# A hybrid block on one core: softplus of later groups summed by transfers, D h and the folding of partial sums left to transfers too, products back with tokens on partitions

## The chip, the cores and the metric

One core of one Trainium2 chip runs the whole program. The metric is the device time of one execution in microseconds, as the median of several runs. All data are fp32. The engines are PE (matrix products; PEld is its weight load), DVE (vector), ACT (scalar functions), POOL (here three kinds of work: a small power, and the issue of most DMAs), and SP (the other DMAs).

## The reference

The input x has 8 batches of 256 tokens with 128 features. Four blocks are added to it one after the other, each on a layer norm of x:

```python
x = x + _L0_attn_a_ref(_layernorm(x), ...)      # a selective-scan (Mamba-like) block
x = x + _L0_ffn_ref(_layernorm(x), ...)         # 8 experts, the best two of each token
x = x + _L0_attn_b_ref(_layernorm(x), ...)      # gated attention with squared relu
x = x + _L0_ffn_ref(_layernorm(x), ...)         # the same experts again
```

In the first block, 256 channels carry a state of 16 numbers each. After a projection, a convolution over 4 tokens and a SiLU that gives `h`, the recurrence is

```python
delta = jax.nn.softplus(ts @ dt_w + dt_b)
...
new = dA * state + d_t[:, :, None] * B_t[:, None, :] * h_t[:, :, None]
y = jnp.einsum('bin,bn->bi', new, C_t) + D * h_t
return (new, y * g_t)
...
return ssm @ out_w + out_b
```

The third block ends with `(u * attn_v) @ W_out + b_out`.

## The kernel before

The 8 batches are cut into four groups (0 to 3) of two batches, 512 tokens each. Most tiles have 128 features on partitions and a group's 512 tokens along the free dimension; x itself is held with tokens on partitions. A group passes through these steps, each a Python generator that yields one operation at a time:

- `prelude(g)` (named s): norm, transposes, projection `hid`, convolution, `h`, the projection `xpj` with B and C (which go through DRAM to be broadcast), and the softplus. That is built as relu(z) + ln(1 + e), e = exp(-|z|), with a correction of the rounding of 1 + e. In the tile `dl`, the relu (L569 on ACT; group 0 on DVE, L565) is joined by the correction (L587, L589) and the logarithm (L597), all on DVE; then `du` = dl * h (L598).
- `recurrence(g)` (m): 8 rounds q of 2 of the 16 state numbers, for each of two halves c of the channels. One such step is three DVE instructions over 128x1024: B du (L703), the scan (L708), times C (L712). ACT makes the decay exp(A delta) ahead (`feeder`, L658), which needs the exp table. From the second round on a step's result `st` is added to the first round's, `acc`, by a DMA that POOL issues (`adder`, L675). There are two `acc` and a ring of three `st`. Group 0's last two are left to PE instead. When all adds have landed, PE sums what is left in PSUM as `y` (L724 to L727): the skip D h by a diagonal matrix `skip_sb`, and each part by the identity; DVE multiplies with the gate into `du` (L730).
- `gating(g)` (g): the gate's projection and SiLU. `tail(g)` (t): `project_back` with `out_w`.
- `rest(g)` (r): experts (p), attention (a), experts again (r). An expert layer goes through 22 tiles of intermediate features: `gp` on PE, SiLU on ACT (`sg`), `up` on PE from x weighted by the token's share of the expert (`wb`), their product `it` on DVE (L925), and `dn` on PE (L931). The share of expert 0 is spread over the partitions by four products with the identity (L861); the others come as broadcast DMAs from DRAM (L894, POOL), followed by a multiplication on DVE (L902). Three `wb` buffers rotate.

`project_back` (and the end of an expert layer) makes features-on-partitions results of 512 columns, `pb`; `add_back` copies them to SBUF on ACT with the bias (`oT`, L451), turns them by four transposes on PE (`ot`, L458), and adds them to x on DVE (L461).

The order of the instructions on each engine is made by hand, before the program is built. Several such generators (lanes) are open at a time. `Board` keeps, in estimated microseconds, when each engine and each tile is free; `pick` takes the lane whose next operation can start first, and among lanes of the same engine that could start within PATIENCE of it the one with the lowest rank (`RANKS`; also estimates like `mm`, `act_us`, 0.2 for a transpose). A change of ACT's function table counts SWITCH more if the operation has been ready for less than LONG; with PATIENCE and LONG both 0 no wait is put up with to save a table load. When PE is expected to idle before a fresh accumulation, `do` writes filler products with the identity, one for each FILL = 0.23 us of the expected idle beyond 0.3 us (L307). Each engine executes its instructions strictly in that order, and waits on semaphores where an input isn't there. A DMA's wait is done by the queue that issues it (POOL or SP), and all that stands behind it on that queue waits too.

```python
for _ in range(int((idle - 0.3) / self.FILL)):
    op.fill()
```

Of the kernel before, what the change touches and what calls it, by code (L numbers as in the profile page):

```python
# [31 lines left out]
class Board:  # L32
# [3 lines left out]
    SWITCH = 1.3  # L36
    PATIENCE, LONG = 0, 0
    FILL = 0.23
# [56 lines left out]
def kernel(  # L95
# [27 lines left out]
    nc = tc.nc  # L123
# [25 lines left out]
    RANKS = {  # L149
        "s": [2, 4, 1.5, 2.5], "m": [3, 3.5, 3, 3.5],  # L150
        "g": [2, 2, 3.5, 2], "t": [1, 0, 3, 0],
        "r": [2.5, 1, 3.5, 1], "feeder": 5, "adder": 2.5,
    }
    SPLIT = ()
    ENDS = 2
# [37 lines left out]
    for name, src in (  # L193
        ("norm_scale", norm_scale.rearrange("(c p) -> c p", p=P)),
        ("in_b", in_b.rearrange("(c p) -> c p", p=P)),
        ("conv_w", conv_w.rearrange("k (c p) -> (k c) p", p=P)),
        ("conv_b", conv_b.rearrange("(c p) -> c p", p=P)),
        ("dt_b", dt_b.rearrange("(c p) -> c p", p=P)),
        ("D", D.rearrange("(c p) -> c p", p=P)),
        ("b_uv", b_uv.rearrange("(c p) -> c p", p=P)),  # L200
        ("gamma", gamma),
        ("beta", beta),
        ("out_b", out_b.rearrange("(c p) -> c p", p=P)),
        ("b_out", b_out.rearrange("(c p) -> c p", p=P)),
    ):
        n = src.shape[0]
        (nc.scalar if nrow % 2 else nc.gpsimd).dma_start(vecs[nrow : nrow + n, :], src)
        rows[name] = nrow
        nrow += n
# [32 lines left out]
    nc.sync.dma_start(b_v, b_uv[SE : 2 * SE].partition_broadcast(P))  # L242

    xs += [load_x(g) for g in range(1, NG)]

# [23 lines left out]
    one = const.tile([P, 1], FP, name="one")  # L269
    nc.vector.memset(one, 1.0)  # L270


# [25 lines left out]
    def shut(*held):  # L298
        for h in held:
            h.open = False  # L300

    def pe(us, out, ins, issue, fresh=True):
        def fill():
            ps = out[0].ap
            ps = ps if len(ps.shape) == 2 else ps.rearrange("p a b -> p (a b)")
            m, n = ps.shape[0], min(P, ps.shape[1])
            nc.tensor.matmul(ps[:, 0:n], lhsT=ident[:, 0:m], rhs=ident[:, 0:n], start=True, stop=True)  # L307

        return Op("PE", us, out, ins, issue, lag=0.25, fill=fill if fresh else None)
# [13 lines left out]
    def mm(n):  # L323
        return 0.06 + 0.00157 * n

# [101 lines left out]
    def transposed(xn, name, xT, scale=None):  # L427

        NT = xn.ap.shape[1]
        ps = bank([P, NT, P], f"tp_{name}")  # L430

        def turn():
            for t in range(NT):
                nc.tensor.transpose(ps.ap[:, t, :], xn.ap[:, t, :], ident)

        yield pe(0.2 * NT, [ps], [xn], turn)
        flat = ps.ap.rearrange("p t q -> p (t q)")
        yield act(act_us(NT * P), [xT], [ps], lambda: (
            nc.scalar.copy(xT.ap, flat) if scale is None else nc.scalar.mul(xT.ap, flat, scale)
        ))  # L440
        shut(ps)

    def add_back(x, psT, name, key, bias=None):
# [15 lines left out]

        yield pe(0.2 * NT, [ps], [oT], turn)  # L460
        yield dve(dve_us(NT * P), [x], [ps], lambda: nc.vector.tensor_add(x.ap, x.ap, ps.ap))  # L461
# [10 lines left out]

    def project_back(x, srcT, w_sb, bias, name, key):

        n = x.ap.shape[1] * P
        ps = bank([P, n], f"pb_{name}")
        yield pe(mm(n) * len(srcT), [ps], srcT, product(
            ps.ap, [(w_sb[:, c, :], s.ap) for c, s in enumerate(srcT)]
        ))
        yield from add_back(x, ps, name, key, bias)  # L480

# [3 lines left out]
    def prelude(g):  # L485

        GB = SIZES[g]
        G = GB * T
        xn = yield from layernorm(Held(xs[g]), f"m{g}", "m", rms=True, parts=xh[g])
        xT = ring(norm, [P, G], "xTm", f"xT_m{g}")  # L490
        yield from transposed(xn, f"m{g}", xT, scale=col("norm_scale"))


# [59 lines left out]

        dl = [ring(mam, [P, G], f"dl{c}", f"dl_{g}_{c}", bufs=2) for c in range(NI)]
        ex = ring(mam, [P, NI, G], "ex", f"ex_{g}")
        for c in range(NI):
# [11 lines left out]
            else:  # L568
                yield act(act_us(G), [dl[c]], [ps], lambda: nc.scalar.activation(  # L569
                    dl[c].ap, ps.ap, AF.Relu, bias=col("dt_b", c)  # L570
                ))
            shut(ps)

        parts = [(c, c + 1) for c in range(NI)] if g == 0 else [(0, NI)]
        exs = [Held(ex.ap[:, a:b, :], ex.ready) for a, b in parts]
# [26 lines left out]
        ww.used = max(w.used for w in wws)  # L602
        led_up[g] = bc, h, xT, dl, du

    def gating(g):
# [17 lines left out]
    fed = {}  # L623
    gone = {"du": 0, "scan": 0, "ct": 0, "sums": 0, "added": 0}
    sums = []

    def feeder():

        for g in range(NG):
# [6 lines left out]
            for q in range(N // NC):  # L636
# [12 lines left out]
                for c in range(NI):  # L649
# [16 lines left out]
                    das.append(da)  # L666

    def adder():

        while len(done & {f"m{g}" for g in range(NG)}) < NG:  # L670
            if not sums:
                yield None
                continue
            acc, st = sums.pop(0)
            yield load(6.3, [acc], [st], lambda: nc.gpsimd.dma_start(  # L675
                acc.ap, st.ap, accum_op=ALU.add
            ), "POOL", 0.9)
            st.used = acc.ready
            gone["added"] += 1

    def recurrence(g):
# [7 lines left out]

        acc, last = [], []  # L690
        for q in range(NQ):
            for c in range(NI):
                if q == 0:
                    st = ring(scan, [P, NC, G], f"acc{c}", f"acc_{g}_{c}")
                    acc.append(st)
                else:
                    while gone["added"] < gone["sums"] - 2:
                        yield None
                    st = ring(scan, [P, NC, G], "st", f"st_{g}_{q}_{c}", bufs=3)
                while len(fed.get((g, q), [[]])[-1]) <= c:  # L700
# [13 lines left out]
                if q == NQ - 1 and g == 0:  # L714
                    last.append(st)
                elif q > 0:
                    sums.append((acc[c], st))
                    gone["sums"] += 1
        while gone["added"] < gone["sums"] or g not in gates:
            yield None  # L720
        for c in range(NI):
            y = bank([P, G], f"y_{g}_{c}")
            parts = last[c : c + 1] + [acc[c]]

            yield pe(mm(G) * (NC * len(parts) + 1), [y], parts + [h[c]], product(
                y.ap, [(skip_sb[:, c, :], h[c].ap)]
                + [(ident, t.ap[:, n, :]) for t in parts for n in range(NC)]  # L727
            ))

            yield dve(dve_us(G), [du[c]], [gates[g][c], y], lambda: nc.vector.tensor_mul(  # L730
                du[c].ap, y.ap, gates[g][c].ap
            ))
            shut(y)

    def tail(g):
        gates.pop(g)
        bc, h, _, delta, du = led_up.pop(g)
        G = SIZES[g] * T
        yield from forked((RANKS["t"][g], g), [
            project_back(  # L740
                xh[g][p], of_part(g, p, du), out_w_sb, col("out_b"), f"m{g}{p}", f"y{p}"
            ) for p in range(len(PARTS[g]))
# [33 lines left out]
    def led_in(g, which, key, p, shared):  # L776
# [18 lines left out]

        yield pe(0.35 * NP, [lg], [xT], logits)

# [10 lines left out]
        if "we" not in shared:  # L808
# [8 lines left out]
            ]  # L817
            shared["wb"] = parted(g, ring(
                ffn, [P, NT * P], f"wb{key}", f"wb_{which}{g}_0", bufs=WB
            ))  # L820
        pair, we, wb = (shared[k][1][p] for k in ("pair", "we", "wb"))

# [32 lines left out]


        ps = bank([P, NP, P], f"we0_{nm}")

# [6 lines left out]

        yield pe(0.26 * NP, [ps], [we], spread)
        yield dve(dve_us(NP * P), [wb], [ps, xT], lambda: nc.vector.tensor_mul(
# [4 lines left out]
    def moe(g, which, key, shared, ends):  # L872
# [3 lines left out]
        G = NT * P  # L876
        xT, we, wb = (whole(*shared[k]) for k in ("xT", "we", "wb"))
        whole(*shared["pair"])
        sgs, wx, its = {}, {0: wb}, {}

# [23 lines left out]
        def up(i, cols_of, sg, wa, wn, it, width):  # L904
# [18 lines left out]

            yield pe(mm(width) + 0.3 * (cut < P), [ps], [wa] if cut >= P else [wa, wn], issue)
            yield dve(dve_us(width), [it], [ps, sg], lambda: nc.vector.tensor_mul(  # L925
# [10 lines left out]
        def tile_of(i):  # L936
# [3 lines left out]
        weT_ps = bank([E * NT, P], f"weT_ps_{nm}")  # L940
        yield pe(0.3, [weT_ps], [we], lambda: nc.tensor.transpose(
            weT_ps.ap, we.ap.rearrange("p e t -> p (e t)"), ident
# [11 lines left out]
        for i in range(LEAD):  # L954
            yield from gate(i)
        for e in range(1, WB):
            yield from fetched(e)
        yield from weighted(1)

# [47 lines left out]
    def attention(g, key, p, shared):  # L1007
# [20 lines left out]
        uT = [shared[f"uT{c}"][1][p] for c in range(NE)]  # L1028
        yield from transposed(xn, nm, xT)

        ps = bank([P, n], f"base_{nm}")
# [76 lines left out]
        for b in range(lo, hi):  # L1108
# [19 lines left out]
            shut(ps)  # L1128
        yield from project_back(xh[g][p], uT, wout_sb, col("b_out"), nm, f"{key}{p}")

# [28 lines left out]
    for g in range(NG):  # L1159
# [5 lines left out]
        waiting[-1].name = f"g{g}"  # L1165
        waiting.append(Lane((RANKS["t"][g], g), tail(g), [f"m{g}", f"g{g}"] + [f"t{g - 1}"] * (g > 0)))
        waiting[-1].name = f"t{g}"
# [59 lines left out]
```

## Time and profile before

| what | us |
|---|---|
| median of 3 runs (776.08 to 777.22) | 776.21 |
| the profiled execution | 775.3 |
| its span, first to last instruction | 773.5 |
| longest on the chain that ended last: `dn_r`, `gp_r`, `dn_p` on PE (10%, 9%, 8%); scan L708 on DVE (3%) | |
| DMA: 85.07 MB in all | |

In the lines below, a row of a group has: line, engine, operation, out<-in, shapes, count | busy us, mean ns of one | idle before it. A matrix product in fp32 leaves two PE records, which overlap their neighbours', so that the mean of one (about 600 ns for 512 columns) isn't its cost; the distance from one start to the next is. Some rows that the change touches:

```
L469 PE MATMUL y<-acc,ident 128*128 128x512 f32 x32 | 15.0, 592 | 0.0
L469 PE MATMUL y<-h,skip_sb 128*128 128x512 f32 x16 | 8.2, 593 | 0.0
L587 DVE SCALAR_TENSOR_TENSOR ex<-ww,ex 128x1024 f32<-128x1024 f32 x3 | 3.6, 1216 | 0.0
L589 DVE TENSOR_TENSOR dl<-dl,ex 128x512 f32<-128x512 f32 x8 | 5.3, 688 | 0.2
L597 DVE TENSOR_TENSOR dl<-dl,ww 128x512 f32<-128x512 f32 x8 | 5.4, 678 | 0.0
L57 ACT ACT_TABLE_LOAD x97 | 124.5, 1283 | 1.7
acc<-st POOLq DMA_DIRECT2D x54, 512.0 KB, 6.4
```

The last is of the table of DMA issues: 54 transfers of 512 KB, median 6.4 us from issue to landing.

### The profile page before, as it was taken

How to read it: one execution, taken by the hardware profiler on the slowest of the kernel's cores; microseconds unless marked ns; L12 is line 12 of the kernel's file. 1: busy time of each engine (PE TensorE's matmuls, PEld its weight loads, DVE VectorE, ACT ScalarE, POOL GpSimd, SP SyncE). 2: the span in 40 equal slices, each digit the busy share in tenths (PEclk: the TensorE clock that was granted, in tenths of full speed). 3: DMA queues.
4: the chain of work that ended last, by engine and by line, in shares of the span. 5: the costliest groups of instructions: out<-in, count | busy, mean ns of one | idle time of the engine just before them, and what ended most of it. 6: DMA issues, size and time to landing. Idle time of an engine off the chain costs nothing.

```text
span 773.5 us, 8167 instructions
## 1 busy us (share of the span) xinstructions
PE 745.8 (96%) x2967; PEld 393.5 (51%) x2967; DVE 565.1 (73%) x824; ACT 442.3 (57%) x580; POOL 108.6 (14%) x157
## 2 busy tenths in 40 slices
PE   4999999996999999999999999999999999999997
PEld 3877996652435754334554444344445434543443
DVE  2599998988997999899769898994642634263332
ACT  4688233797983896896956777742153232522221
POOL 2011110120210231211100222111010101010000
PEclk9999999998999999999999999999999999999999
DMA  8629792395863173847612748563010100011110
GB/s 257 195 71 224 179 227 94 86 212 127 215 157 95 54 175 104 191 121 164 161 30 70 176 122 211 146 146 69 2 41 14 41 29 27 14 29 40 28 42 14
DMA packets 33064, 85.07 MB, mean 110 GB/s; under 512 B 4132, under 2 KB 13952, under 8 KB 33024
## 3 DMA queue, kind: packets, MB, share of 16 engines
q0 software_dynamic: 12640, 43.13, 27.1%
q1 hardware_dynamic: 20336, 41.41, 16.4%
q8 instruction: 23, 0.38, 0.2%
q14 instruction: 17, 0.14, 0.1%
q10 hardware_dynamic: 48, 0.01, 0.0%
HBM read 54.79 MB, written 1.44 MB: 73 GB/s over the span
## 4 chain that ended last, share of the span: by engine, by line
PE 75%; DVE 16%; issue 3%; DMA 2%; ACT 2%; POOL 1%; DVEq 0%; POOLq 0%
PE dn_r L931 10%; PE gp_r L469 9%; PE dn_p L931 8%; PE gp_p L469 7%; PE y L307 7%; PE up_r L911 7%; PE up_p L911 6%; PE y L469 3%; DVE st L708 3%; PE up_r L918 3%; PE up_p L918 2%; DMA wb_p<-wrow_p 2%; DVE acc L708 2%; DVE st L703 2%; PE av_a L1116 1%
## 5 line engine op out<-in xcount | busy, mean ns | idle before, releaser
L708 DVE TENSOR_TENSOR_SCAN st<-decay,st 128x1024 f32<-128x1024 f32 x56 | 128.1, 2288 | 3.2 <-DVE st L703 0.5
L57 ACT ACT_TABLE_LOAD x97 | 124.5, 1283 | 1.7
L885 ACT ACTIVATE sg_r<-gp_r,zero 128x512 f32<-128x512 f32 x88 | 60.0, 685 | 112.0 <-PE gp_r L469 93.4
L658 ACT ACTIVATE decay<-dl,zero,a_sb 128x510 f32<-128x510 f32 x128 | 96.6, 805 | 38.1 <-DVE st L708 35.9
L925 DVE TENSOR_TENSOR it_r<-up_r,sg_r 128x512 f32<-128x512 f32 x88 | 60.1, 685 | 65.4 <-PE up_r L911 39.5
L885 ACT ACTIVATE sg_p<-gp_p,zero 128x512 f32<-128x512 f32 x88 | 59.5, 686 | 78.1 <-PE gp_p L469 49.9
L931 PE MATMUL dn_p<-it_p,wd_sb 128*128 128x512 f32 x176 | 92.2, 610 | 5.6 <-DVE it_p L925 5.6
L931 PE MATMUL dn_r<-it_r,wd_sb 128*128 128x512 f32 x176 | 90.2, 602 | 0.0
L469 PE MATMUL gp_p<-xT_p,wg_sb 128*128 128x512 f32 x176 | 89.9, 598 | 0.0
L469 PE MATMUL gp_r<-xT_r,wg_sb 128*128 128x512 f32 x176 | 89.6, 595 | 0.0
L925 DVE TENSOR_TENSOR it_p<-up_p,sg_p 128x512 f32<-128x512 f32 x88 | 59.8, 683 | 36.7 <-PE up_p L911 18.2
L675 POOL DMA_DIRECT2D acc<-st x54 | 47.3, 876 | 238.0 <-DVE st L712 213.1
L712 DVE TENSOR_TENSOR st<-st,ct 128x1024 f32<-128x1024 f32 x56 | 68.3, 1219 | 0.7
L703 DVE TENSOR_TENSOR st<-bt,du 128x1024 f32<-128x1024 f32 x56 | 68.1, 1216 | 0.0
L911 PE MATMUL up_p<-wb_p,wu_sb 128*128 128x512 f32 x128 | 65.5, 595 | 0.0
L911 PE MATMUL up_r<-wb_r,wu_sb 128*128 128x512 f32 x128 | 64.9, 594 | 0.0
L931 PEld LDWEIGHTS dn_p<-it_p,wd_sb 128*128 128x128 f32 x176 | 31.3, 191 | 49.8 <-issue 32.7
L469 PEld LDWEIGHTS gp_r<-xT_r,wg_sb 128*128 128x128 f32 x176 | 33.0, 190 | 43.3 <-issue 38.0
L469 PEld LDWEIGHTS gp_p<-xT_p,wg_sb 128*128 128x128 f32 x176 | 33.5, 192 | 42.0 <-issue 36.2
L307 PEld LDWEIGHTS y<-ident 128*128 128x128 f32 x468 | 52.7, 192 | 1.3 <-PE dt L469 0.8
L307 PE MATMUL y<-ident 128*128 128x128 f32 x468 | 53.0, 275 | 0.0
L931 PEld LDWEIGHTS dn_r<-it_r,wd_sb 128*128 128x128 f32 x176 | 31.5, 190 | 39.7 <-issue 36.1
(226 smaller groups left out, 904.2 us busy)
## 6 DMA issues: line engine op xcount, KB each, us to landing
acc<-st POOLq DMA_DIRECT2D x54, 512.0 KB, 6.4
bt<-bc SPq DMA_DIRECT2D x32, 512.0 KB, 5.9
ct<-bc SPq DMA_DIRECT2D x32, 512.0 KB, 4.6
wb_p<-wrow_p POOLq DMA_DIRECT2D x28, 256.0 KB, 4.0
wb_r<-wrow_r POOLq DMA_DIRECT2D x28, 256.0 KB, 3.6
wg_sb<-in_L_ffn_w_gate_dram SPq DMA_DIRECT2D x2, 704.0 KB
wu_sb<-in_L_ffn_w_up_dram SPq DMA_DIRECT2D x2, 704.0 KB, 5.9
wd_sb<-in_L_ffn_w_down_dram SPq DMA_DIRECT2D x2, 704.0 KB
```

Of the source, the lines that this page charges most:

```text
L57: self.load_tables(op.table)
L307: nc.tensor.matmul(ps[:, 0:n], lhsT=ident[:, 0:m], rhs=ident[:, 0:n], start=True, stop=True)
L469: nc.tensor.matmul(ps, lhsT=lhsT, rhs=rhs, start=(i == 0), stop=(i == len(terms) - 1))
L658: nc.scalar.activation(shaped[:, n, :, 1:], delta[c].ap.rearrange("p (b t) -> p b t", b=GB)[:, :, 1:], AF.Exp, bias=zero, scale=a_sb[:, c, ...
L675: yield load(6.3, [acc], [st], lambda: nc.gpsimd.dma_start(acc.ap, st.ap, accum_op=ALU.add), "POOL", 0.9)
L703: yield dve(1.22, [st], [bt, du[c]], lambda: nc.vector.tensor_mul(st.ap, bt.ap, du[c].ap.unsqueeze(1).to_broadcast([P, NC, G])))
L708: yield dve(2.29, [st], [das[c]], lambda: nc.vector.tensor_tensor_scan(flat, das[c].ap.rearrange("p n t -> p (n t)"), flat, 0.0, ALU.mult, ...
L712: yield dve(1.22, [st], [ct], lambda: nc.vector.tensor_mul(st.ap, st.ap, ct.ap))
L885: yield act(act_us(G), [sg], [gp], lambda: nc.scalar.activation(sg.ap, gp.ap, AF.Silu, bias=zero), SILU)
L911: nc.tensor.matmul(ps.ap, lhsT=wu_sb[:, i * P : (i + 1) * P], rhs=wa.ap[:, cols_of], start=True, stop=True,)
L925: yield dve(dve_us(width), [it], [ps, sg], lambda: nc.vector.tensor_mul(it.ap, ps.ap, sg.ap[:, cols_of]))
L931: yield pe(mm(dn.ap.shape[1]), [dn], [it], lambda: nc.tensor.matmul(dn.ap, lhsT=wd_sb[:, i, :], rhs=it.ap[:, cols_of], start=(i == 0), sto ...
```

## The change

1. In groups 1 to 3 the softplus is put together by two adding DMAs into one tile `both`: the correction `ex` and the logarithm `ww` are added to the relu by POOL's queue. ACT's identity now subtracts one and turns the sign, so that DVE makes the correction in one operation and the logarithm takes the scale -1.
2. In the same groups, ACT multiplies `h` by D in place after `du`, and a DMA of 256 KB adds it to the first state of `acc`. PE's skip product stays in group 0 alone.
3. In groups 2 and 3 (FOLD) a DMA adds the second half of each `acc` to the first, and DVE multiplies it with the gate from SBUF. Group 1 still sums its two halves on PE.
4. What stood at the end of `recurrence` becomes a lane of its own, `ending` (f), so that the next recurrence may begin before it. `acc` and `st` come from one pool of five states.
5. `project_back` makes its products with tokens on partitions: 8 products of 128 columns with the activations as weights, whose sum is added to x directly. `oT` and `ot` are gone there (not at the end of the expert layers). The biases are added to x early by POOL (`biased`), from two tiles that SP loads ahead of the x of groups 1 to 3.
6. The spread of expert 0's share by PE is kept only where SOON names the layer (p0, p1, r0, p3, r3); in p2, r1 and r2 it comes as a DMA like the others.
7. The planner: PATIENCE 0.21, LONG 3.0, new ranks, and new estimates for PE (`mm`, transposes 0.115 each, logits 0.205, spread 0.235, split `up` +0.14).

```diff
-    PATIENCE, LONG = 0, 0
+    PATIENCE, LONG = 0.21, 3.0
...
+        "s": [4, 1, 2.5, 2.5], "m": [1.5, 4, 3.5, 3.5],
+        "g": [4, 0, 3.5, 0], "t": [1, 3, 0, 0.5],
+        "r": [2.5, 1, 3.5, 3], "f": [1, 0, 0.5, 0], "feeder": 5, "adder": 0,
...
+    SOON = ("p0", "p1", "r0", "p3", "r3")
...
-        return 0.06 + 0.00157 * n
+        return 0.005 + 0.00167 * n
...
+    def biased(x, bias):
...
+        yield pool(1.2, [x], [], lambda: nc.gpsimd.tensor_tensor(
+            x.ap, x.ap, bias.unsqueeze(1).to_broadcast([P, NT, H]), ALU.add
...
+    def project_back(x, srcT, w_sb, name):
...
+            for t in range(NT):
+                for c, s in enumerate(srcT):
+                    nc.tensor.matmul(
+                        ps.ap[:, t, :], lhsT=s.ap[:, t * P : (t + 1) * P], rhs=w_sb[:, c, :],
+                        start=(c == 0), stop=(c == len(srcT) - 1),
+                    )
...
+        yield dve(dve_us(NT * P), [x], [ps], lambda: nc.vector.tensor_add(x.ap, x.ap, ps.ap))
...
+            yield act(act_us(NI * G), [ww], [ex], lambda: nc.scalar.activation(
+                ww.ap, ex.ap, AF.Identity, bias=minus_one, scale=-1.0
+            ))
+            yield dve(dve_us(NI * G), [ex], [ww], lambda: nc.vector.scalar_tensor_tensor(
+                ex.ap, ww.ap, 1.0, ex.ap, ALU.add, ALU.add
+            ))
+            sums.append((f"s{g}", 6.3, both, ex, both.ap, ex.ap))
+            yield act(act_us(NI * G), [ww], [], lambda: nc.scalar.activation(
+                ww.ap, ww.ap, AF.Ln, bias=zero, scale=-1.0
+            ), EXP)
+            sums.append((f"s{g}", 6.3, both, ww, both.ap, ww.ap))
+            while landed.get(f"s{g}", 0) < 2:
+                yield None
...
+                yield act(act_us(G), [h[c]], [], lambda: nc.scalar.mul(h[c].ap, h[c].ap, col("D", c)))
...
+                elif g > 0:
+
+                    sums.append((g, 4.5, acc[c], h[c], acc[c].ap[:, 0, :], h[c].ap))
...
+    FOLD = (2,3,)
+
+    def ending(g):
...
+        if g in FOLD:
+            for c in range(NI):
+                sums.append((g, 4.5, acc[c], acc[c], acc[c].ap[:, 0, :], acc[c].ap[:, 1, :]))
+                count += 1
+        while landed.get(g, 0) < count or g not in gates:
             yield None
         for c in range(NI):
+            if g in FOLD:
+                yield dve(dve_us(G), [du[c]], [gates[g][c], acc[c]], lambda: nc.vector.tensor_mul(
+                    du[c].ap, acc[c].ap[:, 0, :], gates[g][c].ap
+                ))
+                shut(acc[c])
+                continue
...
+            skip = [(skip_sb[:, c, :], h[c].ap)] if g == 0 else []
...
+        if not ahead:
+            yield from fetched(0)
```

## The prediction

> **What bounds the kernel now.** I read the page first. PE is busy 96% of the span, but line L307 is among its largest groups, and L307 is filler: products with the identity that the planner writes ahead of a PE operation it expects to wait (0.23 us of expected idle each). So I cut the span into five stages at landmarks of PE's timeline: the router weights of the first expert layer (p0) turned (151.8), p0's result turned back (239.9), the shares of p1 spread (271.2), group 3's product with `out_w` (540.6), the end. The first fence is the page, the second the table by stage (busy time and instruction count of each engine, granted clock, DMA share), the third the same for L307 alone.
>
> ```profile
> PE 745.8 (96%) x2967; PEld 393.5 (51%) x2967; DVE 565.1 (73%) x824; ACT 442.3 (57%) x580; POOL 108.6 (14%) x157
> ```
> ```profile
> 0.00:151.80 151.80, 139.40 (x953) 114.40 (x954) 122.32 (x152) 83.59 (x118) 19.77 (x40) 1.00 0.63 165
> 151.80:239.90 88.10, 78.90 (x246) 33.82 (x246) 78.68 (x75) 74.12 (x85) 15.78 (x21) 0.96 0.74 179
> 239.90:271.20 31.30, 30.25 (x159) 21.49 (x158) 27.98 (x66) 21.71 (x29) 6.34 (x4) 1.00 0.17 48
> 271.20:540.60 269.40, 268.68 (x871) 120.15 (x870) 237.25 (x316) 191.85 (x240) 48.06 (x64) 1.00 0.56 135
> 540.60:773.50 232.90, 228.60 (x748) 103.66 (x746) 98.87 (x218) 71.02 (x109) 18.60 (x29) 1.00 0.09 27
> ```
> ```profile
> 0.00:151.80 151.80, 96.99 (x831) 96.30 (x832) 1.00 0.63 165
> 151.80:239.90 88.10, 6.19 (x51) 6.09 (x52) 0.96 0.74 179
> 239.90:271.20 31.30, 8.22 (x68) 8.01 (x68) 1.00 0.17 48
> 271.20:540.60 269.40, 6.96 (x58) 6.95 (x58) 1.00 0.56 135
> 540.60:773.50 232.90, 1.32 (x8) 1.12 (x8) 1.00 0.09 27
> ```
>
> The reader is to see that until 271 PE waits for others (filler, and idle that shows at 151.8 to 239.9, where DVE and ACT are busiest), and that from 271 on PE is full of real work.
>
> PE executes its queue in order, filler included, so I count it. The timeline of PE gives the cadence: a product over 512 columns (two records) starts 0.86 us after the last, four transposes take 0.44, four 128-column products (eight records) 0.89, a filler 47.84/213 = 0.224.
>
> ```profile
> 441.87 0.60 PE L458 MATMUL ot_r<-ident,oT_r 128*128 128x128 f32 x4
> 442.31 1.02 PE L931 MATMUL dn_r<-it_r,wd_sb 128*128 128x512 f32 x2
> 443.17 1.02 PE L469 MATMUL gp_r<-xT_r,wg_sb 128*128 128x512 f32 x2
> 444.03 1.02 PE L911 MATMUL up_r<-wb_r,wu_sb 128*128 128x512 f32 x2
> ...
> 462.05 1.05 PE L861 MATMUL we_p<-ident,we_p 128*128 128x128 f32 x8
> 462.94 1.02 PE L911 MATMUL up_r<-wb_r,wu_sb 128*128 128x512 f32 x2
> ```
>
> At these cadences (256 columns 0.43, a split `up` 0.99) the program before holds 609.5 us of real PE work and 507 fillers, 112.9. The span of 773.5 leaves 51.1 in which PE does nothing: 19.1, 15.0, 2.5, 6.0 and 8.5 by stage. PE's share is therefore sharp; only the 51.1 must be guessed.
>
> **The change on PE.** The programs' order of instructions gives the counts. Sums of groups (`y`): 28 products of 512 columns become 14 (no D h in groups 1 to 3, no `y` in groups 2 and 3): -12.0. The transposes after `pb_m` and `pb_a` go, 32 at 0.11: -3.5. The products back become 64 of 128 columns (64 x 0.2225 = 14.2) for 16 of 512 (13.8): +0.5. Three of the eight spreads of the first share (L861) become transfers, 12 x 0.2225: -2.7. Real work 591.8, so -17.7. But the new planner writes 561 fillers, 54 more: 54 x 0.2225 = +12.0. They are executed whether or not the wait comes. Net -5.7. By stage, real + filler, before to after: 132.7 to 130.2; 73.1 to 69.6; 28.8 to 39.4; 263.4 to 264.2; 224.4 to 213.3.
>
> **The change elsewhere.** DVE loses, in each of groups 1 to 3, two subtractions and two additions of 512 columns (L589, L597: 688 and 678 ns), 2.7 us each; adds from PSUM after the products back replace those after the transposes, one for one. One such 2.7 us lies in stage 1 and one in stage 2, where DVE ends the waits; the third lies under PE. ACT loses 26 of 98 table loads at 1283 ns (33 us, from PATIENCE and LONG) and eight copies `oT` (687 ns), and gains six products h D (0.69, the row of the same shape). Ten of the loads and four decay instructions leave stage 2.
>
> Stage 2 is where this pays. The order before puts 14 recurrence steps there (1.22 + 2.29 + 1.22 = 4.73 us of DVE each), the new one 12: DVE 78.7 - 9.5 - 2.7 = 66.5, ACT 74.1 - 12.8 - 3.2 + 1.4 = 59.5, PE 69.6. The stage took 9.4 more than its busiest engine; 69.6 + 9.4 = 79.0. With the PE idle of 15.0 kept it is 84.6. I take 80, near the first, since every engine has slack then. What leaves is late next in stage 3: there the order shows 72 fillers for 34, ahead of `tp_a` and `we_p`, as I read it because the moved recurrence steps no longer cover p0's serial end and attention's start.
>
> Sum: stage 1 130.2 + 19.1 = 149.3; stage 2 80; stage 3 39.4 + 2.5 = 41.9; stage 4 264.2 + 6.0 = 270.2; stage 5 213.3 + 8.5 = 221.8. Together 763.2.
>
> **What before does not show.** (a) Eight adds of a bias on POOL, 128x512. From below the affine select of 128x128 on POOL, 285 ns, times 4 = 1.1 us; from above that plus the slowest row of POOL's tensor_tensor, 1727 ns (four elements, a power): 2.9. They wait for the last reader of x, and behind them stand adds and loads of the same queue. POOL is 14% busy; I take 0 for the end, at worst five of them (before 272) at 2.9 = 14.5. (b) Softplus: per group two adds of 512 KB to one tile. The second waits for the first to land (rows `acc<-st`: 4.5/6.4/9.8 us least, median, most), so POOL stands up to 9 us; behind it are queued the add of a recurrence state and, in stage 2, `wb_p` for expert 5. The order places the products du two to four steps later, and wb_p 5 is first read five rounds after its buffer comes free (5 x 80/22 = 18 us), so I take 0; at worst 9 each in stages 1 and 2, if DVE runs out of the five states. (c) D h by transfer is issued at a group's first step and hidden by the other seven. The folding add of groups 2 and 3 (256 KB; rows 3.3 to 9.2) comes after the last add and ahead of `du`; group 2's hides behind p1 and r0, group 3's tail is what the fillers of stage 5 (38 for 4) stand for. Counted. Removing everything could also pull stage 1 in by the slack of the recurrence's start (DVE waited 3.2 us for `y`), a gain of up to 3. (d) Traffic grows by 3 + 2.5 + 0.75 = 6.3 MB on 85.1.
>
> For all of these I add 1: 764.2. The profiled execution took 775.3 with a span of 773.5 (+1.8), and the median is 0.9 above it: **767**.
>
> [...] DVE's products with both operands in SBUF fill these stages (L703 and L712 1.22 us). [...]
>
> **The rivals.** *The relief goes further* (chance 0.18, 757): stage 2 comes down to 73 and attention starts before its fillers are through; 767 - 7 for the stage, - 3 for (c). For it: ACT loses 14.6 us there. Against: PE alone has 69.6.
>
> *The fillers do not replace idle, they are added to it, and the transfers are late* (0.14, 775): the 51.1 stays (span 767.8, so 770.5), plus one late wait of 4 to 5. For it: stage 5 was full of real work, and 38 fillers now stand in it. Then the change does little, 775 against 776.2.
>
> *Slower: POOL's queue stops the expert layers* (0.16, 782). The place is stage 2, later r0 and p1. Before, two late inputs there already cost PE this:
>
> ```profile
> 177.31 1.05 PE L918 MATMUL up_p<-wb_p,wu_sb 128*32 128x512 f32 x2 [3.37 <-DVE wb_p L902]
> ...
> 187.73 2.08 PE L931 MATMUL dn_p<-it_p,wd_sb 128*128 128x512 f32 x2 [3.92 <-DVE it_p L925]
> 189.60 1.91 PE L469 MATMUL gp_p<-xT_p,wg_sb 128*128 128x512 f32 x2
> 191.44 1.66 PE L918 MATMUL up_p<-wb_p,wu_sb 128*32 128x512 f32 x8
> ```
>
> After the second pause a product takes 1.87 (187.73 to 189.60) for 0.86, until 193.04, and the clock column falls to 0.96: 2.9 more. Together 3.4 + 3.9 + 2.9 = 10.2. The pair of softplus adds sits in the same queue as `wb_p` at the same place, with DMA already at 0.74. One more such burst brings 777, no change; the case decides from there, at one and a half it is 782, at two 787. Against: the landings of 8 to 9 us that caused it are already in the stage.
>
> **How the numbers follow.** Forecast 767 (0.52, 761 to 773). Within 0.2% of 776.2 (774.7 to 777.8) is about what a measurement of this kernel can't tell from no change. Faster: forecast 0.52 + relief 0.18 + 0.06 of the little case = 0.76; same 0.08; slower 0.16. The range 757 to 780 leaves out half of the relief case and most of the slow one, some 0.2, and reaches over the worst of (a) (767 + 13).
>
> **What would show it.** The span less real PE work and fillers stays near 50, with stage 2 at 77 to 85 us; the lines that follow L587 to L597 keep group 0's work and one operation for each later group; `y` keeps 14 products; table loads 72; no row in which ACT or DVE waits long for `dl`. Wrong would be: waits of `it` or `up` for `wb` beyond the 3.4 and 3.9 of before, DVE's first product of a step waiting for a landing, a POOL bias add over 3 us, or the clock column below 0.96 outside stage 2.

## The result and the profile after

The changed kernel takes 777.47 us (median of 12 runs, 772.93 to 779.3), the kernel before beside it 776.6 (775.1 to 777.37): ratio 1.0005, 95% interval 0.9986 to 1.0024. That is no change; 767 was forecast. The execution profiled after took 779.3 (span 777.3), the upper end of its runs, so its stages show some 2 us more than a median run would.

The first fence is the page's line of engines, the second the table by stage at the same landmarks as before (busy time and count of each engine, granted clock, DMA share), the third the fillers alone (now L326).

```profile
PE 744.7 (96%) x3087; PEld 404.9 (52%) x3087; DVE 567.4 (73%) x813; ACT 408.9 (53%) x552; POOL 136.0 (17%) x183
```
```profile
0.00:154.60 154.60, 138.47 (x940) 113.89 (x941) 122.08 (x148) 84.42 (x119) 27.34 (x46) 0.99 0.67 173
154.60:238.10 83.50, 75.73 (x232) 31.75 (x231) 69.00 (x67) 59.77 (x73) 15.85 (x21) 0.96 0.74 170
238.10:280.20 42.10, 41.79 (x261) 32.97 (x260) 38.83 (x80) 25.10 (x34) 13.49 (x9) 1.00 0.47 112
280.20:555.20 275.00, 270.97 (x892) 121.07 (x892) 242.38 (x310) 172.91 (x224) 57.91 (x75) 1.00 0.62 144
555.20:777.30 222.10, 217.76 (x771) 105.18 (x769) 95.14 (x210) 66.73 (x103) 21.40 (x32) 1.00 0.11 29
```
```profile
0.00:154.60 154.60, 94.68 (x810) 93.93 (x810) 0.99 0.67 173
154.60:238.10 83.50, 5.17 (x42) 5.19 (x43) 0.96 0.74 170
238.10:280.20 42.10, 16.98 (x144) 16.74 (x144) 1.00 0.47 112
280.20:555.20 275.00, 6.73 (x50) 6.52 (x50) 1.00 0.62 144
555.20:777.30 222.10, 9.64 (x76) 9.27 (x76) 1.00 0.11 29
```

The reader is to see that the work fell nearly as forecast (in stage 2 DVE from 78.7 to 69.0, with 66.5 forecast, ACT from 74.1 to 59.8, with 59.5 forecast), and that stage 2 still takes 83.5. Counted as in the prediction, real PE work is 591.7 us (forecast 591.8) and filler 124.5 (124.9). But the time in which PE does nothing grew from 51.1 to 61.1: by stage from 19.1, 15.0, 2.5, 6.0, 8.5 to 24.8, 14.0, 2.6, 10.8, 8.8. Stages 3 and 5 came out at 42.1 and 222.1 (forecast 41.9 and 221.8); stage 1 is 5.3 over the forecast, stage 2 3.5, stage 4 4.8.

This is one execution. Two runs below, x3 and f2, have the same instructions in the same order through stages 1 to 3; they took 154.4 and 155.2 in stage 1, 80.9 both in stage 2, 42.1 and 42.2 in stage 3. So the miss of stage 1 is firm, and that of stage 2 lies between 0.9 and 3.5.

What POOL's queue does in stage 1 is the next view, its timeline (start, time, what it waited for).

```profile
77.09 0.86 POOL L748 DMA_DIRECT2D dl<-ex  x1 [0.28 <-DVE ex L620]
86.47 0.86 POOL L748 DMA_DIRECT2D dl<-ww  x1 [8.52 <-ACT decay L729]
87.02 2.10 POOL L748 DMA_DIRECT2D st<-st  x2
96.71 0.87 POOL L748 DMA_DIRECT2D st<-st  x1 [7.59 <-DMA st<-st]
```

The second softplus transfer stands 8.5 us, until the first has landed (8.9 us from its issue), and the state adds leave behind it, two at once. (The releaser printed is ACT, whose `ww` was done at 78.0; the time is that of the landing. At 202.3 the same wait of 7.63 is printed as ended by DMA `dl<-ex`.) DVE, in order, then misses first `dl`, then a free state:

```profile
92.00 1.29 DVE L633 TENSOR_TENSOR du<-dl,h 128x512 f32<-128x512 f32 x2 [0.91 <-DMA dl<-ww]
96.20 1.23 DVE L776 TENSOR_TENSOR st<-bt,du 128x1024 f32<-128x1024 f32 x1 [2.90 <-DMA st<-st]
```

PE, which sums group 0's states at the end of this stretch, waits 4.3 us for one of them, and its products are slow behind that (5.34 us for eight records, 3.70 in x1 below; granted clock 0.86 from 120 to 132):

```profile
120.30 5.34 PE L488 MATMUL y<-st,ident 128*128 128x512 f32 x8 [4.25 <-DVE st L785]
```

The same stand is there at 193.8 (7.6 us) and 323.9 (7.6). In stage 2 PE's long pause is one of 5.7 us (3.4 and 3.9 in the kernel before), and slow products follow it (a product over 512 columns each 1.87 to 1.6, for 0.86):

```profile
179.88 1.93 PE L1025 MATMUL up_p<-wb_p,wu_sb 128*32 128x512 f32 x8 [5.71 <-DVE it_p L1032]
181.75 2.08 PE L1038 MATMUL dn_p<-it_p,wd_sb 128*128 128x512 f32 x2
183.62 1.75 PE L488 MATMUL gp_p<-xT_p,wg_sb 128*128 128x512 f32 x2
```

This pause ends at 179.9, ahead of the stand at 193.8, which so has no part in it; in x3 and f2 it is 4.3 and 4.0.

And a bias add on POOL stretches what DVE does beside it: the scan of 2.29 us takes 3.18.

```profile
46.66 1.65 POOL L495 TENSOR_TENSOR x<-x,b_first 128x512 f32<-128x512 f32 x1 [3.40 <-ACT xn_m L438]
```
```profile
47.27 3.18 DVE L781 TENSOR_TENSOR_SCAN st<-decay,st 128x1024 f32<-128x1024 f32 x1
```

The end of the scan less 2.29 is 48.16; POOL's add ends at 48.31. As an estimate from these two rows, the scan did next to nothing until the add was through. Six DVE instructions are stretched so, by some 6.5 us in all; in each, the end less the usual length falls 0.13 to 0.25 us ahead of the add's end.

### The profile page after: what moved, and what is told of

Same layout as the page of the kernel before. It is cut to its first block, busy times and chain, and to the rows that moved or that the text cites. A ratio compares the mean times of both kernels' runs of the same rounds, so it can differ in the third digit from the quotient of the medians.

```text
span 777.3 us, 8439 instructions
## 1 busy us (share of the span) xinstructions
PE 744.7 (96%) x3087; PEld 404.9 (52%) x3087; DVE 567.4 (73%) x813; ACT 408.9 (53%) x552; POOL 136.0 (17%) x183
## 3 DMA queue, kind: packets, MB, share of 16 engines
q0 software_dynamic: 15152, 49.69, 31.8%
## 4 chain that ended last, share of the span: by engine, by line
PE 56%; DVE 14%; DMA 13%; issue 5%; POOL 1%; ACT 1%; POOLq 0%; DVEq 0%
PE dn_r L1038 8%; PE gp_r L488 8%; PE dn_p L1038 7%; PE up_r L1018 6%; PE gp_p L488 5%; DMA wb_p<-wrow_p 5%; PE up_p L1018 5%; DVE st L781 3%; PE up_r L1025 3%; DVE st L776 2%; PE up_p L1025 2%; DVE st L785 2%; DMA st<-st 2%; DMA dl<-ex 2%; DMA wb_r<-wrow_r 2%
## 5 line engine op out<-in xcount | busy, mean ns | idle before, releaser
L781 DVE TENSOR_TENSOR_SCAN st<-decay,st 128x1024 f32<-128x1024 f32 x64 | 147.9, 2311 | 3.2
L748 POOL DMA_DIRECT2D st<-st x58 | 52.1, 920 | 229.0 <-DVE st L785 201.2
L776 DVE TENSOR_TENSOR st<-bt,du 128x1024 f32<-128x1024 f32 x64 | 77.9, 1218 | 2.9 <-DMA st<-st 2.9
L785 DVE TENSOR_TENSOR st<-st,ct 128x1024 f32<-128x1024 f32 x64 | 79.0, 1234 | 1.0
L326 PEld LDWEIGHTS y<-ident 128*128 128x128 f32 x414 | 46.6, 192 | 1.3 <-PE dt L488 0.8
L326 PE MATMUL y<-ident 128*128 128x128 f32 x414 | 46.8, 275 | 0.0
```

The costliest lines, as they stand in the source:

```text
L748: yield load(us, [acc], [st], lambda: nc.gpsimd.dma_start(into, of, accum_op=ALU.add), "POOL", 0.9)
L776: yield dve(1.22, [st], [bt, du[c]], lambda: nc.vector.tensor_mul(st.ap, bt.ap, du[c].ap.unsqueeze(1).to_broadcast([P, NC, G])))
L781: yield dve(2.29, [st], [das[c]], lambda: nc.vector.tensor_tensor_scan(flat, das[c].ap.rearrange("p n t -> p (n t)"), flat, 0.0, ALU.mult, ...
L785: yield dve(1.22, [st], [ct], lambda: nc.vector.tensor_mul(st.ap, st.ap, ct.ap))
```

## Theories

T: POOL's queue, standing 8 us for the second softplus transfer, makes states, `wb` and `du` late. R1: the bias adds cost, by DVE. R2: the 54 new fillers are pure cost. All experiments change the kernel after and keep the order of all other instructions, unless it is said. The stages are lengths in us of the profiled execution, at the same landmarks; the time is a median; the ratio is to the kernel before. Each stage length is of one execution: by the 83.5, 80.9 and 80.9 above, a difference of under 3 us in stage 2 shows little by itself, and the 12 runs of the kernel after spread over 6.4 us.

| run | stages 1, 2, 3, 4, 5 | time | ratio (95%) |
|---|---|---|---|
| after | 154.6, 83.5, 42.1, 275.0, 222.1 | 777.47 | 1.0005 (0.9986–1.0024) |
| x1 no softplus transfers | 149.7, 78.8, 42.2, 279.3, 222.1 | 773.67 | 0.9961 (0.9948–0.9974) |
| x2 no biases | 151.6, 79.7, 41.9, 274.5, 222.1 | 771.84 | 0.9950 (0.9938–0.9961) |
| x3 no late fillers | 154.4, 80.9, 42.1, 274.9, 226.3 | 780.78 | 1.0055 (1.0043–1.0068) |
| x4 all three | 149.0, 76.2, 41.8, 277.2, 226.4 | 773.80 | 0.9972 (0.9962–0.9982) |
| e1 no transfers, no biases | 148.7, 78.9, 41.8, 277.8, 222.2 | 770.66 | 0.9925 (0.9914–0.9937) |
| f1 one transfer | 153.9, 79.7, 42.1, 275.7, 222.2 | 775.39 | 0.9983 (0.9975–0.9992) |
| f2 all spreads on PE | 155.2, 80.9, 42.2, 278.7, 222.6 | 781.02 | 1.0052 (1.0035–1.0069) |
| f3 f1, biases on PE | 154.9, 78.6, 44.3, 279.8, 222.2 | 780.20 | 1.0047 (1.0033–1.0060) |
| f4 f3, all spreads | 154.1, 78.9, 44.3, 280.8, 222.6 | 784.12 | 1.0103 (1.0088–1.0117) |
| h1 softplus on DVE | 151.7, 80.0, 42.2, 279.5, 222.1 | 777.39 | 1.0019 (1.0009–1.0029) |
| h2 h1, biases on DVE | 158.3, 78.1, 44.1, 278.6, 222.5 | 783.58 | 1.0095 (1.0081–1.0109) |
| h3 h1, biases by transfer | 150.4, 79.7, 43.4, 274.7, 222.1 | 771.47 | 0.9935 (0.9921–0.9949) |
| h4 h2, 14 fillers | 157.4, 81.3, 43.9, 278.5, 222.5 | 785.14 | 1.0113 (1.0099–1.0127) |
| e2 biases by transfer | 152.1, 79.9, 42.0, 274.8, 222.1 | 773.24 | 0.9964 (0.9953–0.9975) |
| e3 h3, 14 fillers | 150.6, 82.5, 41.8, 276.6, 222.1 | 774.77 | 0.9971 (0.9960–0.9982) |
| e4 h3, `wb` first | 150.3, 80.0, 41.9, 273.7, 222.1 | 769.34 | 0.9908 (0.9896–0.9920) |

## Leaving the suspects out

x1, the softplus transfers:

```diff
-            yield load(us, [acc], [st], lambda: nc.gpsimd.dma_start(
+            yield load(us, [acc], [st], lambda: str(g).startswith("s") or nc.gpsimd.dma_start(
```

> The changed kernel without the six accumulating transfers of the softplus (dl <- ex, dl <- ww of groups 1 to 3 are not issued, so the two terms of softplus that they carry are left out); the order of all other instructions stays. Theory T (POOL's queue stands some 8 us three times while the second add waits for the first to land, and what is queued behind it, state adds and wb, comes late): the idle time of PE falls from 61.1 us to 50 to 54, stage 1 from 154.6 to 149 to 151, stage 4 from 275.0 to 270 to 272, DVE's waits of wb_p for a landing from 23.9 us to under 12; time 767 to 771. Rival R1 (the bias adds on POOL stretch DVE's instructions): less than 2 us gained, 775 to 778. Rival R2 (the late fillers are pure cost): no gain either, 775 to 778.

Stages 1 and 2 gained 4.9 and 4.7, to 149.7 and 78.8, beside forecasts of 149.3 and 80. T holds in stage 1: DVE waits neither for `dl` nor for a state any more, and of PE's wait 0.2 is left:

```profile
116.09 3.70 PE L488 MATMUL y<-st,ident 128*128 128x512 f32 x8 [0.24 <-DVE st L785]
```

In stage 2 the gain is 2.1 beside the 80.9 of the other executions, which is within their scatter. DVE's waits for `wb_p` came down from 23.9 to 14.1, not to under 12; in x3 and f2 they are 20.4 and 14.9 with the transfers kept. The time, 773.67, lies between T's range and that of the rivals, for stage 4 lost 4.3, which no theory expected. In its PE timeline the pause before the first `up_r` of group 1's second expert layer is 3.6 us (1.4 in the kernel after), and slow products follow it (1.86 and 1.71 from one start to the next, for 0.86):

```profile
428.43 2.07 PE L1018 MATMUL up_r<-wb_r,wu_sb 128*128 128x512 f32 x2 [3.64 <-DVE wb_r L1009]
430.29 1.91 PE L488 MATMUL gp_r<-xT_r,wg_sb 128*128 128x512 f32 x2
```

x2, the biases:

```diff
-        yield pool(1.2, [x], [], lambda: nc.gpsimd.tensor_tensor(
-            x.ap, x.ap, bias.unsqueeze(1).to_broadcast([P, NT, H]), ALU.add
-        ))
+        yield pool(1.2, [x], [], lambda: None)
```

> The changed kernel without the eight bias adds on POOL (both biases left out); the order of all other instructions stays. R1 (the bias adds stretch DVE's scans and products by some 6.5 us in all, and hold POOL's queue): 4 to 6 us gained, 771 to 773, with no scan above 2.4 us where a bias add ran. T: 0 to 2 us gained, 775 to 777, since stages 1 and 4 keep POOL's waits for dl <- ex. R2: nothing, 777.

5.6 us gained, at the upper end of R1's range; the scan at 45.6 takes 2.29 again. Stage 1 gives 3.0. Stage 2 gives 3.8, though no bias add lies in it: its pause is 3.0 instead of 5.7, but 2.6 of the 3.8 are what the same instructions differ by between executions.

x3, the late fillers (`fill` returns after its 498th call):

> The changed kernel with the 63 fillers after the start of the second attention layer not issued (498 of 561 stay); the order of all other instructions stays. R2 (these fillers are added to the idle time instead of standing in for it): 63 x 0.2245 = 14 us less, 762 to 765. T (most of them stand where PE would wait anyway): 2 to 6 us gained, 771 to 775, with PE's idle time after 238 us grown by 8 to 12 us. Were the clock to fall for want of them, slower than 778 with a granted clock below 0.99 after 280 us. R1: as T.

R2 is refuted for the late fillers: 3.3 us slower, the expectation's third case. (The 38 that are new in stage 3 were not left out.) Stage 4, with 25 fillers less, is unchanged; stage 5, with 38 less, is 4.2 longer. The windows of PE from 552 to 592, of this kernel and of the kernel after, show why (the last but two is the granted clock):

```profile
552.00:592.00 40.00, 33.47 (x122) 20.65 (x121) 19.26 (x62) 14.76 (x24) 6.59 (x8) 0.83 0.06 18
```
```profile
552.00:592.00 40.00, 39.89 (x207) 27.75 (x206) 21.76 (x68) 15.14 (x24) 6.60 (x8) 1.00 0.07 21
```

Without the fillers PE pauses 3.3 us at 554.7, and then runs at about half its pace until 571.9 (`base_a` to `v_a` 1.87 us for 0.97). The 38 fillers stand in for idle time, and with them the clock here is 1.00 for 0.83.

x4, the three edits together, and e1, the first two with all fillers kept:

> The changed kernel without the six transfers of the softplus, the eight bias adds and the 63 late fillers together (softplus terms and biases left out). If the costs are separate, the gains of the three runs before add up: by T 7 + 1 + 4, so 763 to 767; if all three theories hold in full, 8 + 5 + 14, 750. If a fourth cause is the larger one, less than 5 us is gained, 772 or more.

> The changed kernel without the softplus transfers and without the bias adds, all fillers kept (softplus terms and biases left out); the order of all else stays. If the transfers of the softplus and the bias adds are the whole of what the prediction missed, the stages come to its numbers: stages 1 to 3 at 149 + 76 + 42, stage 4 at 270 to 276, stage 5 at 222, so a span of 759 to 765 and a time of 761 to 767. If something else stops PE too (the late wb_r before the second expert layer of group 1, 3.8 us in the run without the transfers), stage 4 stays at 277 to 280 and the time at 766 to 770.

x4 fell outside both sums and into the last case (773.8): it also loses in stage 5, as x3 (226.4 and 226.3 for 222.1; mean clock of the execution 0.986 and 0.981 for 0.992). e1 says more: 770.66, its span 769.4 for the 764.2 worked out. Its stages 1, 2, 3 and 5 are below the forecast ones or within 0.4 of them (148.7, 78.9, 41.8, 222.2 beside 149.3, 80, 41.9, 221.8); the rest is stage 4, 277.8 for 270.2. So the two left-out things make up the miss in stages 1 to 3, nearly all of it in stage 1, and a third thing is in stage 4.

## Putting the work elsewhere

f1, one transfer in place of two:

```diff
+                if str(g).startswith("s") and landed.get(g, 0) == 0:
+                    held[g] = of
+                    return
+                if g in held:
+                    nc.vector.tensor_add(of, of, held.pop(g))
+                nc.gpsimd.dma_start(into, of, accum_op=ALU.add)
```

> The changed kernel with one transfer per group for the softplus: DVE adds the logarithm to the other term in SBUF (1.4 us for 1024 columns, three times), and the sum goes to dl by a single accumulating transfer, issued where the second stood; all other instructions keep their order. Theory T (the cost is POOL standing some 8 us for the landing of the first add): no DMA issue on POOL waits for dl <- ex any more; stages 1 and 2 together fall from 238.1 us to 229 to 232, as without the transfers (228.5) plus at most the two DVE adds; time 771 to 775, stage 4 between 271 and 280 by whether wb_r comes late there. Rival (it is the traffic of the softplus transfers or their place, not the wait): stages 1 and 2 stay above 235 and the time at 775 to 779.

2.1 us less. Stages 1 and 2 sum to 233.6, between T's 229 to 232 and the rival's 235. Stage 1 falls only to 153.9: POOL waits 9.6 us for DVE's sum instead, two state adds are still issued together behind it, and DVE waits 2.3 for a state. Half of the softplus traffic is gone and most of stage 1's loss is still there, which speaks for the stand and against the traffic.

h1, no transfer, both adds on DVE:

```diff
...
+                else:
+                    nc.vector.tensor_add(of, of, held.pop(g))
+                    nc.vector.tensor_add(into, into, of)
```

> The changed kernel with the softplus of groups 1 to 3 put together on DVE at the place of the second transfer (two adds of 1024 columns, 2 x 1.2 us in each of three groups) and no transfer for it; all other instructions keep their order. Theory T (POOL's queue and the late landings, not the work that DVE was relieved of, cost the time): DVE waits neither for dl nor for a state at 92 to 96 us; stage 1 at 151 to 153, as without the transfers (149.7) plus the adds, stage 2 at 79 to 81, time 771 to 775. Rival (the relief of DVE was worth what the change wanted, and the adds now cost the scan 2.4 us in each of stages 1 and 2 and more behind them): 776 to 779.

Stages 1 and 2 fall to 151.7 and 80.0, within T's ranges, though DVE has the work back. The time does not fall (777.39), as the rival said, but not for its reason: stage 4 is 4.5 longer, with a pause of 3.7 before the same `up_r`. In x1, x4, e1, h1, h2 and h4 that pause is 3.4 to 3.8; in after, x2, x3, f1, f3, h3, e2 and e3 1.0 to 1.5. POOL's timeline, here of x1, tells them apart:

```profile
419.21 0.88 POOL L748 DMA_DIRECT2D st<-st  x1 [5.96 <-DVE it_r L1032]
419.75 2.00 POOL L1001 DMA_DIRECT2D wb_r<-wrow_r  x3
```

Three `wb_r` loads stand behind a state add. In the long cases the add is released with DVE's next `it_r` (after 6.0 us), in the short ones with the state's own product (5.1). `wb_r` leaves 0.9 us later, beside SP's 512 KB load `bt`, and lands 2 us later. Why the release moves is not settled.

f2 returns the three spreads of first shares to PE (`SOON` names all eight layers; replanned):

> The changed kernel with the first shares of all eight expert layers spread by PE again (the three that the change gave to transfers are taken back: 12 products of 128 columns, 2.7 us of PE); written by the same planner, so the order after 390 us differs a little. Theory W (the three transfers make PE wait 1.5 us and more for the first up of the second expert layer of group 1 and the first of group 2, rows at 434.2 and 468.5): the two waits go, 3 us against 2.7, and the time stays within 775.5 to 778.5. Rival (PE has no slack there, the waits are only moved): 779 to 781.

The waits at 434 and 468 go, but another of 2.0, with 1.9 lost in slow products behind it, ends at 476.2; 781.02, as the rival had it. In f4, with f3's edits, that wait is 2.1, at full pace behind it:

> One transfer for the softplus, three first biases by PE, and all eight first shares spread by PE. T and W: the sum of the three, 766 to 771, so faster than both kernels; with the waits in stage 4 near 433 and 467 us gone and PE's idle time at 48 to 52 us. Rival: as the third kernel of this set or 1 to 3 us slower, since the spreads cost PE 2.7 us in its full stretch.

784.12. The expectation failed with f3, whose bias goes through PE:

```diff
+                if bias is not None:
+                    nc.tensor.matmul(
+                        ps.ap[:, t, :], lhsT=ones_row, rhs=bias[0:1, :], start=True, stop=False
+                    )
...
```

> As the kernel with one transfer, and the first bias of groups 0, 1 and 2 is added by PE in front of the product back (12 products of 1 row by 128 columns, 12 x 0.11 = 1.3 us) instead of by POOL; all other instructions keep their order. If the POOL adds in stage 1 cost what leaving all eight out gained there (3.0 of 154.6 us), it is 2 to 4 us faster than the kernel with one transfer: 767 to 772. Rival (the gain of leaving the biases out came from the five other adds or from chance in where PE pauses): within 1.5 us of the kernel with one transfer.

```profile
256.33 0.48 PE L507 MATMUL pb_m<-b_first,ones_row 1*128 1x128 f32 x2
256.75 0.71 PE L511 MATMUL pb_m<-out_w_sb,du 128*128 128x128 f32 x4
```

A one-row product and the two after it start 1.06 us apart (256.33 to 257.39 to the next), where the two alone took 0.44 (f1: 16 records from 256.43 to 258.21): 0.62 for what was counted at 0.11. By that, twelve cost an estimated 7.4 instead of 1.3. In stage 4 the granted clock fell too behind four of them (0.86 over 406 to 418), with PE busy for 11.9 of these 12 us. This run says nothing for or against R1.

h2 has the biases on DVE (`nc.gpsimd` to `nc.vector` in L495):

> As the kernel with the softplus on DVE, and the eight bias adds on DVE too, at the same places (8 x 0.7 us). R1 (a bias add on POOL stretches the DVE instruction beside it by 0.9 to 1.8 us and holds POOL's queue 1.3 to 3.2 us): 1 to 4 us faster than the kernel before it in this set. Rival (the eight adds cost DVE the same 5.5 us in another form): within 1 us of it.

```profile
22.76 0.69 DVE L495 TENSOR_TENSOR x<-x,b_first 128x512 f32<-128x512 f32 x1 [14.71 <-DMA b_first<-in_L_attn_a_out_b_dram]
```

6.2 us slower than h1. The first add stands 14.7 us at the head of DVE's queue for the bias itself, which SP loads late (issued at 17.7 in the kernel after); on POOL the same wait of 16.2 held nothing of weight (its next instruction came at 41.4). Stage 1 is 6.6 longer.

h3 and e2 have them by transfer, with and without h1's edit:

```diff
-        yield pool(1.2, [x], [], lambda: nc.gpsimd.tensor_tensor(
-            x.ap, x.ap, bias.unsqueeze(1).to_broadcast([P, NT, H]), ALU.add
+        yield pool(1.2, [x], [], lambda: nc.gpsimd.dma_start(
+            x.ap, bias.unsqueeze(1).to_broadcast([P, NT, H]), accum_op=ALU.add
```

> As the kernel with the softplus on DVE, and the eight biases added to x by accumulating transfers (256 KB each) from the same place in POOL's queue, so neither POOL nor DVE computes them. R1: the stretched DVE instructions are gone, 3 to 5 us faster than the kernel with the softplus on DVE. Rival (2 MB more in the accumulating queue delay the state adds and wb, which landed in 5 to 9 us): no faster, or up to 5 us slower.

> The changed kernel with the eight biases added by accumulating transfers (256 KB each) from the same places of POOL's queue, the softplus transfers kept. R1 (the bias adds on POOL cost by the DVE instructions beside them): as much gained as by leaving the biases out, 771 to 774. If the gain of the kernel with both edits came from the softplus as well: 774 to 777. If the traffic counts: 777 or more.

e2 gains 4.2 us on the kernel after, within R1's range, though the queue carries 2 MB more (51.79 MB for 49.69): the scan at 47.2 takes 2.29. h3 gains 5.9 on h1 (1.3 of it in stage 1, 4.8 in stage 4, where the short pause came, less 1.2 in stage 3, where the granted clock was 0.66 from 263 to 268) and beats both kernels.

h4 and e3 put 14 fillers ahead of one `up` of the first expert layer, to see whether they shorten PE's long pause of stage 2 (5.7 us in the kernel after) and whether the slow products behind it go:

> As the kernel with the softplus and the biases on DVE, and 14 products with the identity (14 x 0.22 = 3.1 us) ahead of the sixth up of the first expert layer, where PE paused 3 to 6 us in every run and ran at half its pace for up to 4 us behind the pause. [...] Rival (the pause is bound by the landing of wb_p alone and what follows would have waited anyway): within 0.7 us of the second kernel of this set.

> The kernel with the softplus on DVE and the biases by transfer, and 14 products with the identity (3.1 us) ahead of the third up of the first expert layer, the one before which PE paused 3 to 6 us near 170 us in every run (the earlier try had them ahead of the sixth, where PE does not wait). [...] Rival (the inputs behind the pause are late as well): no change, 771 to 772.

h4 had them at a place where PE does not wait, and just paid for them: stage 2 is 3.2 longer than in h2, the time 1.6. In e3 the fillers write into the tile of the `up` behind them, whose wait ends with DVE's `it` (5.71 us in the kernel after), so by the author's reading they ran after the pause, in place of the slow products. Stage 2 is 2.8 us longer than in h3, the time 3.3. A shorter pause there is no sure cure either: in x4 it was 2.2, and slow products followed (granted clock 0.79 over 168 to 176).

e4 is h3 with the held-back state adds:

```diff
...
+                if (g, landed.get(g, 0)) in LATER:
+                    late.append((into, of))
...
+                while e == WB - 1 and late:
+                    a, b = late.pop(0)
+                    nc.gpsimd.dma_start(a, b, accum_op=ALU.add)
```

> The same kernel (softplus on DVE, biases by transfer) with four state adds moved behind the first wb loads of the first expert layer of group 0 (two adds), the second of group 1 and the first of group 2. If what is left of PE's pauses at 170, 428 and 462 us is POOL's order (a 512 KB add queued ahead of wb), the three pauses of 4.7, 1.2 and 1.6 us shrink to under 1 each, and the slow products behind the first go: 764 to 768. Rival (the adds then come late and the five states run out): the gain is eaten, 769 to 774.

The pauses at 428 and 462 are gone, and stage 4 is 273.7, the shortest of all runs:

```profile
428.54 1.02 PE L1033 MATMUL up_r<-wb_r,wu_sb 128*128 128x512 f32 x2
```

In stage 2 the rival is right: `wb` lands early (in 4.6 us, for 9.4 in h3), but DVE now waits for a state that the late adds keep, and PE's pause stays 3.9.

```profile
166.68 1.23 DVE L787 TENSOR_TENSOR st<-bt,du 128x1024 f32<-128x1024 f32 x1 [6.07 <-DMA st<-st]
```

769.34, at the edge of the rival's range, is the best here, 0.9% below the kernel before.

## Why the prediction was wrong

The step that failed is that (a) and (b) were both taken at 0. Stage 1 shows it: 149.3 forecast, 154.6 measured, and 148.7 with both left out (e1). Stage 4 held a second failure: 270.2 forecast, 275.0 measured.

- **The change on PE, real and filler**: right to 0.4 us. So were table loads (72, as forecast) and DMA volume (91.8 MB for 91.4). Stages 3 and 5 within 0.3, and x3 shows that the fillers of stage 5 stand for idle, as read.
- **(b), softplus: failed.** "So I take 0": the stand was seen (up to 9 us; measured 8.5, 7.6, 7.6), but its price was taken as hidden by the five states. They ran out in stage 1. x1 prices it: 4.9 in stage 1, and in stage 2 4.7 beside the profiled execution but 2.1 beside the 80.9 of the others, each within the bound of 9 that was kept for the range.
- **(a), the biases: failed.** Taken at 0; a bias add took 1.26 to 3.17 us, and e2 and x2 price the eight at 4.2 and 5.6 of the end. Six DVE instructions beside the adds took some 6.5 us more, the scan 3.18 for 2.29. The 0 was the author's estimate: the kernel before has no POOL add of 128x512, so no row of it shows one beside a DVE instruction.
- **The change on PE, the spreads: failed in part.** Three spreads were priced as 2.7 us saved. Given to POOL's queue they also made PE wait 1.4 and 1.3 before the `up` at 436 and 470 in the kernel after, and 3.4 to 3.8 before the first of these in six others. e4, which reorders the queue, does away with both pauses; f2, which takes the spreads back, is 3.5 us slower: 2.7 of PE's work is back, and another pause comes.
- **The allowance of 1 us for all unknowns** was too small by 13.1 us of span. e1, without (a) and (b), takes back 7.9; the other 5.2 lie in stage 4 (+7.6, less 1.4 in the others and the 1 us).
- **The slower rival** named the right queue, but not the place: the long pause of stage 2 (5.7, and 4.3 and 4.0 in the same instructions) is little longer than the 3.9 of before, and stage 1, which it did not name, lost more.
- **The rival with the fillers** came nearest in number (775), by luck: the 51.1 did not stay but grew to 61.1, and x3 shows that the late fillers replace idle.
- **Of the signs of being wrong** three came true: a pause above 3.9, a product of DVE that waits for a landing (2.9), a bias add over 3 us (3.17).
- Two slips in the working change nothing: the slow products before cost 2.6, not 2.9 (5.31 us from 187.73 to 193.04, for 2.71 at full pace), and the worst of (a), 14.5, goes beyond the range's 767 + 13.

What stays open: why the state add ahead of `wb_r` is released 0.9 us later in some kernels, and how much of stage 4's other idle time is the kernel's order.

## What to carry to other kernels

Two accumulating transfers to one tile in one in-order queue cost the landing of the first here (POOL stood 8.5, 7.6 and 7.6 us), and what was queued behind paid (two state adds left together at 87.0); price such a wait by what it starves (a ring of buffers, a load), not by the tile it is for. An engine called idle is not free if its instructions hold up those of the bound engine (POOL, 17% busy, and the scan's 3.18 for 2.29), and a removed cause may return its gain at a later pause, which can cost PE its pace as well (x1 lost 4.3 us in stage 4, with a pause of 3.6 and products 1.86 apart for 0.86). How far a stage differs between executions of the same instructions (2.6 us here) bounds what one profile of each kernel can show.

## What was not expected of the hardware

- After most of PE's longer pauses a product over 512 columns took about 1.87 us for 0.86 (before at 187.73, after at 179.88, x1 at 428.43), for 3.5 us (h2, 182.2 to 185.7) to 14 us (x3, 557.9 to 571.9). The length of the pause alone does not decide: slow products followed pauses of 2.0 (f2) and 2.2 (x4), none followed 3.4 in the kernel before (at 177.31) or 3.6 in f4 (at 118.7, granted clock 1.00 from 110 to 130). In h3 the clock fell near 264 while PE was busy throughout (0.66 from 263 to 268).
- A one-row product of 128 columns cost 0.62 us among full products in f3, where a full one takes 0.22.
- In the kernel after a 512 KB accumulating transfer to `dl` landed 7.9 to 8.9 us after its issue, the next one to the same tile in 4.7 to 5.5.
